# A DCNv3 layer ahead of an attention layer: position weights summed on GpSimd, and a new order of the work

## The chip, the cores and the metric

The kernel runs on one core of a Trainium2 chip. The time is the device time of one execution in microseconds (us). Three executions of the kernel before took 3407.39, 3409.13 and 3413.03 us, with a median of 3409.13 us. A core has five engines, each with a queue that it works through in order: TensorE (PE in the profile; its weight loads are PEld), VectorE (DVE), ScalarE (ACT), GpSimd (POOL) and SyncE (SP), which here issues most DMAs.

## The reference, cut to what matters

An image batch `x` of 2 x 512 x 64 x 64 floats goes through two layers, each added to its input. Layer 0, which alone is changed, is a deformable convolution (DCNv3) on the group-normed `x`:

```python
xproj = inp @ in_w + in_b                          # 512 -> 512, per pixel
x1 = conv 3x3, one filter per channel, of inp      # "depthwise", 9 taps
x1 = gelu(layernorm over the 512 channels(x1))
offset = x1 @ off_w + off_b                        # 16 groups x 9 points x 2
mask = softmax(x1 @ mask_w + mask_b over 9 points)
out = for each pixel and group: sum over 9 points of
      mask * bilinear sample of xproj at (point + offset)
x = x + out @ out_w + out_b
```

Layer 1 is full attention over 4096 pixels with 512 channels; the diff leaves it alone.

## The kernel before

**What is computed how.** Offsets are taken to stay below one pixel in size, so each sample reads at most a 5 x 5 neighbourhood. For each pixel and group the nine bilinear samples are therefore one weighted sum over 25 neighbours. These 25 *position weights* are what `weights` builds in the tile `aw` (128 pixels x 5 x 5 x 64, the 64 being 4 pixel blocks x 16 groups). Should an offset be larger, another path (not run here) recomputes everything.

**Chunks and stages.** Layer 0 works on 16 chunks of 512 pixels (8 rows of one image). Each chunk `i` goes through four stages, written as Python generators; a `yield` ends a step:

- `project(i)`: reads rows (SP), normalizes them on ACT into `xn` (one copy, 4 channel blocks `kb`), and multiplies by `in_w` on PE (`pq`, L789, 4 tiles), copied out by ACT (`xj`, L795).
- `features(i)`: the depthwise convolution. The first tap of each of the 4 channel blocks is an ACT instruction (L814); the other 8 x 4 taps are DVE `scalar_tensor_tensor` instructions (L820) that add to the tile `conv`. POOL sums the 4 blocks (L829, L831: `tot`), PE turns the sum into a mean over channels (`p_mean`, L836), DVE subtracts it (L841), ACT squares, POOL sums the squares (L847, L849: `sq`), PE takes the variance, ACT the root, DVE the reciprocal (L855) and product (L856), ACT the gelu (L860).
- `weights(i)`: PE multiplies by the offset and mask weights (`po`, L877, 4 tiles), DVE adds the bias into `o` (L882), ACT takes exp (L889), DVE forms the bilinear factors `tx` (L894, L895), ACT a relu that checks offsets (L901, it overwrites `o[:, 0:2]`), DVE the softmax sum and product (L904 to L909) and `my` (L912). Then come nine points: the first product goes straight into `aw`; each of the other eight is a DVE product into `pk` (L920, 128 x 576) and a DVE addition of `pk` into a 3 x 3 window of `aw` (L925). ACT copies all of `aw` into `at` in one instruction (L928), PE transposes it in 16 pieces (`p_tr`, L936) and ACT copies these to `awT` (L937).
- `sample(i)`: PE spreads the weights over the neighbourhood (`pb`, L965), ACT copies them to `bt` (L970), PE does the weighted sums (`pa`, L984), ACT copies them (`dT`, L995), PE multiplies by `out_w` (`py`, L1004, 4 tiles); DVE adds the input (`res`, L1009) and takes statistics for layer 1 (L1010).

**The order.** Inside `manual_schedule` the program's order is each engine's order. `period` writes the order of one round by hand: it interleaves `sample(i)` (called `m`), the tail of `sample(i-1)` (`y`), `weights(i+1)` (`w`), `features(i+2)` (`f`) and `project(i+3)` (`p`), the last transposes of `weights(i)` (`v`), and the first taps of `features(i+3)` (`g`). `more` takes one step of the statistics of image 1, whose input ACT fetches by DMA (L731, L744). Ahead of the 16 rounds stands the *fill*: stages of chunks 0, 1 and 2 in an order of their own. Chunks 14 and 15 have `next_to_last` and `last_period`.

**Buffers that matter.** In the pool of small tiles every tag has one buffer, so `pk` is one tile and `tot`, `sq` and `rstd` share another. PSUM tiles of the tag `mm` (`pq`, `py`, `po`, `p_tr`, `p_mean`) take turns in four buffers.

Of the kernel before, what the change touches and what calls it, by code (L numbers as in the profile page):

```python
# [13 lines left out]
ALU = mybir.AluOpType  # L14
# [515 lines left out]
LEAD = 4  # L530
SCORE_MAX = 6.0
# [43 lines left out]
def window_path(ctx: ExitStack, tc: tile.TileContext, t_in: dict, out: bass.AP, far: bass.AP, sums: bass.AP):  # L575
# [67 lines left out]
    with ExitStack() as l0:  # L643
# [111 lines left out]
        def project(i):  # L755
# [5 lines left out]
            raws = deque()  # L761

# [8 lines left out]
            for kb in range(3):  # L771
                read(kb)
# [5 lines left out]
            for kb in range(KB):  # L778
                nc.scalar.activation(
                    xn[:, kb, r0 : r0 + hi - lo, :], raws.popleft(),  # L780
                    AF.Identity, bias=bi[:, kb : kb + 1], scale=sc[:, kb : kb + 1],
                )
                if kb + 3 < KB:
                    read(kb + 3)
                yield
# [16 lines left out]
        def features(i):  # L802
# [9 lines left out]
            for kb in range(KB):  # L812
                dst, src, wt = tap_of(kb, 1)
                nc.scalar.activation(dst, src, AF.Identity, bias=dw_b[:, kb : kb + 1], scale=wt)  # L814
                if i < 2 or kb == KB - 1:
                    yield
            for kb in range(KB):
                for tap in (0, 2, 3, 4, 5, 6, 7, 8):
                    dst, src, wt = tap_of(kb, tap)
                    nc.vector.scalar_tensor_tensor(dst, src, wt, dst, ALU.mult, ALU.add)  # L820
                    if tap < 8:
                        yield

                if kb == 1:
                    if i == 1:
                        tot = io.tile([P, ROWS + 2, W], F32, name="raw", bufs=3).rearrange("p r c -> p (r c)")[:, :CH]
                    else:
                        tot = sm.tile([P, CH], F32, tag="tot", name="tot")
                    nc.gpsimd.tensor_add(tot, a[:, 0, :], a[:, 1, :])  # L829
                elif kb > 1:  # L830
                    nc.gpsimd.tensor_add(tot, tot, a[:, kb, :])  # L831
                yield

            def mean_over_c(tot):
                p = ps.tile([P, CH], F32, tag="mm", name="p_mean")
                nc.tensor.matmul(p, ones, tot, start=True, stop=True)  # L836
                return p

            mu = mean_over_c(tot)
# [3 lines left out]
            for kb in range(KB):  # L843
                nc.scalar.activation(f[:, kb, :], a[:, kb, :], AF.Square)
                if kb == 1:
                    sq = sm.tile([P, CH], F32, tag="tot", name="sq")
                    nc.gpsimd.tensor_add(sq, f[:, 0, :], f[:, 1, :])  # L847
                elif kb > 1:
                    nc.gpsimd.tensor_add(sq, sq, f[:, kb, :])  # L849
            yield  # L850
            var = mean_over_c(sq)
# [16 lines left out]
        def weights(i):  # L868
# [5 lines left out]
            for t in range(4):  # L874
                po = ps.tile([P, CH], F32, tag="mm", name="po")
                for kb in range(KB):
# [3 lines left out]
                    )  # L880
                yield
# [34 lines left out]
            for k in (4, 0, 1, 2, 3, 5, 6, 7, 8):  # L916
                kx, ky = divmod(k, 3)
                dst = aw[:, ky : ky + 3, kx : kx + 3, :]
                pk = dst if k == 4 else sm.tile([P, 3, 3, 4 * G], F32, tag="pk", name="pk")
# [4 lines left out]
                if k != 4:  # L924
                    nc.vector.tensor_add(dst, dst, pk)  # L925
                yield
            at = sm.tile([P, G, 4, 32], F32, tag="tx", name="at")
            nc.scalar.copy(  # L928
                at.rearrange("p g t w -> p w t g")[:, :NW], aw.rearrange("p y x (t g) -> p (y x) t g", t=4)
            )  # L930
            yield
# [101 lines left out]
        def period(y, v, m, w, f, g, p, more, last):  # L1033
# [5 lines left out]
            p()  # L1039
            y()  # L1040
            v(4)
            more()
            f(4)
            more()
            y()
            for taps in (9, 7, 6, 6):
                m(2)
                w()
                f(taps)
                w()  # L1050
                if taps in (7, 9):
                    more()
# [4 lines left out]
            f()  # L1057
            y()
            f()
# [8 lines left out]
            w(2)  # L1068
# [7 lines left out]
            for k, steps in enumerate((1, 2, 2, 2)):  # L1076
# [7 lines left out]
                if k == 2:  # L1084
                    more()
                if k < 3 and (k or not last):
# [3 lines left out]
                if k == 2:  # L1090
                    g()
            w()

        def next_to_last(y, v, m, w):

            y()
            w(8)
            v(4)
# [7 lines left out]
            w(2)  # L1106
# [54 lines left out]
        with tc.manual_schedule():  # L1161
# [7 lines left out]
            for t in range(4):  # L1169
                p0(2)  # L1170
                f0(8)
            border()
            more()
            p1(3)
            f1()
            next(products)
            p1()
            f1(2)
            next(products)
            p1()  # L1180
            f1()
            f1(6)
            f0(2)
            p1(4)
            f1(12)
            f0()
            p1(2)
            f0()
            p1()
            f0(2)  # L1190
            p1()
            f1(14)
            next(products)
            p2(5)
            f()
            for t in range(4):
                v()
                more()
                more()
                v()  # L1200
            fetch(0, 0)
            fetch(0, 1)
            f1()
            v()
            f1()
            v()
            p2(2)
            v(2)
            p2(2)
            v()  # L1210
            f1()
            v(3)
            p2(2)
            f1()
            p2()
            f1(2)
            p2()
            v(6)
            next(products)
            run(output_bias())  # L1220
            v()
            for i in range(NSEQ):
# [11 lines left out]
                period(y, v, m, w, f, g, Chain(project, i + 3), more, i + 3 == NSEQ)  # L1234
# [652 lines left out]
```

## Time and profile before

The profiled execution took 3413.08 us, and 3411.3 us of it lie between its first and last instruction. So it stands 3.95 us above the median of the three timed executions.

| stretch of the span | us | PE busy | DVE busy | ACT busy | POOL busy |
|---|---|---|---|---|---|
| fill, 20.0 to 158.9 | 138.9 | 91.7 | 119.2 | 55.9 | 29.1 |
| round with statistics of image 1, 230 to 301 | 71.0 | 66.2 | 66.6 | 53.9 | 13.0 |
| plain round, 646.8 to 714.5 | 67.7 | 64.5 | 62.7 | 53.9 | 13.1 |
| last rounds, 1125.1 to 1220 | 94.9 | 84.7 | 50.7 | 50.7 | 1.2 |
| layer 1, 1220 to 3411.3 | 2191.3 | 2071.2 | 1687.3 | 496.7 | 220.8 |

The instruction `my` (L912) stands once in each chunk; its starts lie 62.9, 70.8, 70.9, 71.3, 69.9, nine times 67.7 and 50.3 us apart. Where a row of the trace gives a start and a duration, the first number is the start in us from the span's beginning. A text in brackets is the idle time of the engine ahead of the instruction, with what ended it. "Busy" PE includes matmuls that stand in its pipeline, so a PE at 95% still has room.

### The profile page before, as it was taken

How to read it: one execution, taken by the hardware profiler on the slowest of the kernel's cores; microseconds unless marked ns; L12 is line 12 of the kernel's file. 1: busy time of each engine (PE TensorE's matmuls, PEld its weight loads, DVE VectorE, ACT ScalarE, POOL GpSimd, SP SyncE). 2: the span in 40 equal slices, each digit the busy share in tenths (PEclk: the TensorE clock that was granted, in tenths of full speed). 3: DMA queues.
4: the chain of work that ended last, by engine and by line, in shares of the span. 5: the costliest groups of instructions: out<-in, count | busy, mean ns of one | idle time of the engine just before them, and what ended most of it. 6: DMA issues, size and time to landing. Idle time of an engine off the chain costs nothing. (4 is left out here: it accounts for less than half of the span.)

```text
span 3411.3 us, 38291 instructions
## 1 busy us (share of the span) xinstructions
PE 3152.2 (92%) x14147; PEld 2265.2 (66%) x14147; DVE 2755.0 (81%) x3826; ACT 1349.5 (40%) x1802; POOL 435.7 (13%) x474
## 2 busy tenths in 40 slices
PE   5789999999999899899999999999899999999990
PEld 2355555555555567687787877887587787787880
DVE  8899999998999568786885976968697696885975
ACT  2477788788877533202213112023211202203105
POOL 2112111211121001001001010000101101001112
PEclk9799999999999999999999999999999999999995
DMA  6333443344333268758658667657866758658788
GB/s 227 104 99 116 136 125 111 93 127 128 101 97 117 98 233 268 235 181 236 190 167 222 197 192 207 202 189 247 256 196 193 208 185 236 185 170 223 240 296 356
DMA packets 238388, 629.98 MB, mean 185 GB/s; under 512 B 28112, under 2 KB 45136, under 8 KB 237168
## 3 DMA queue, kind: packets, MB, share of 16 engines
q1 hardware_dynamic: 181456, 431.07, 37.8%
q0 software_dynamic: 43936, 159.40, 18.0%
q10 hardware_dynamic: 12800, 36.97, 3.0%
q8 instruction: 114, 1.87, 0.2%
q14 instruction: 82, 0.67, 0.1%
HBM read 410.15 MB, written 124.91 MB: 157 GB/s over the span
## 5 line engine op out<-in xcount | busy, mean ns | idle before, releaser
L1501 PE MATMUL accy<-tt,v 128*128 128x256 f32 x2016 | 601.3, 380 | 0.8 <-DVE ct L1530 0.6
L1413 ACT ACTIVATE e<-pS 128x1024 f32<-128x1024 f32 x256 | 248.3, 1021 | 727.2 <-PE pS L1408 723.0
L1501 PE MATMUL accx<-e,v 128*128 128x256 f32 x1792 | 471.6, 386 | 0.0
L1501 PE MATMUL accy<-e,v 128*128 128x256 f32 x1792 | 461.3, 380 | 0.0
L820 DVE SCALAR_TENSOR_TENSOR conv<-xn,L_conv_dw_w_sb,conv 128x504 f32<-128x504 f32 (+1 forms) x512 | 409.4, 808 | 37.5 <-ACT conv L814 23.6
L1501 PEld LDWEIGHTS accy<-tt,v 128*128 128x128 f32 x2016 | 384.3, 191 | 53.8 <-DVE ct L1530 1.0
L1501 PEld LDWEIGHTS accx<-e,v 128*128 128x128 f32 x1792 | 334.2, 191 | 120.8 <-issue 80.6
L1501 PEld LDWEIGHTS accy<-e,v 128*128 128x128 f32 x1792 | 342.2, 191 | 46.1
L1480 DVE TENSOR_TENSOR tt<-e 128x256 f32<-128x256 f32 x448 | 187.7, 419 | 178.5 <-PE accy L1501 149.6
L1481 DVE TENSOR_TENSOR tt<-tt,e 128x512 f32<-128x512 f32 x448 | 310.0, 692 | 15.3
L1501 PE MATMUL accx<-tt,v 128*128 128x256 f32 x1008 | 301.3, 381 | 5.1 <-DVE tt L1480 5.1
L984 PEld LDWEIGHTS pa<-bt,patch 96*128 96x128 f32 x2048 | 249.6, 196 | 57.5 <-issue 34.9
L1408 PE MATMUL pS<-q,keys 64*128 64x512 f32 x1024 | 257.9, 623 | 15.3 <-ACT e L1413 15.3
L984 PE MATMUL pa<-bt,patch 96*128 96x128 f32 x2048 | 253.5, 281 | 7.7 <-ACT bt L970 6.3
L970 ACT COPY bt<-pb 96x1024 f32<-96x1024 f32 x124 | 235.1, 2009 | 58.1 <-PE pb L965 58.1
L789 PE MATMUL pq<-in_w,xn 128*128 128x512 f32 x512 | 240.5, 614 | 6.8 <-DVE o L882 4.6
L1004 PE MATMUL py<-dT,L_conv_out_w_sb 128*128 128x512 f32 x512 | 236.6, 607 | 4.8 <-ACT dT L995 4.8
L1506 ACT COPY u<-accx 128x256 f32<-128x256 f32 x56 | 20.8, 372 | 519.7 <-PE accx L1501 517.0
L1501 PEld LDWEIGHTS accx<-tt,v 128*128 128x128 f32 x1008 | 192.2, 191 | 32.0 <-DVE tt L1480 6.3
L877 PE MATMUL po<-om_w_pg,feat 128*128 128x432 f32 x512 | 204.8, 546 | 2.3 <-ACT feat L860 2.3
L995 ACT COPY dT<-pa 32x256 f32<-32x256 f32 x496 | 179.6, 362 | 66.0 <-PE pa L984 56.7
L1422 POOL DMA_DIRECT2D tot<-e x144 | 124.0, 887 | 583.5 <-DVE e L1398 277.7
(242 smaller groups left out, 4331.4 us busy)
## 6 DMA issues: line engine op xcount, KB each, us to landing
v<-wv SPq DMA_DIRECT2D x436, 448.0 KB
tot<-e POOLq DMA_DIRECT2D x176, 512.0 KB, 7.0
patch<-xt SPq DMA_DIRECT2D x256, 192.0 KB
v<-ww SPq DMA_DIRECT2D x56, 448.0 KB
wv<-vform SPq DMA_DIRECT2D x48, 512.0 KB
wv<-vsum SPq DMA_DIRECT2D x48, 384.0 KB
xt<-xj SPq DMA_DIRECT2D x128, 128.0 KB
res<-in_x SPq DMA_DIRECT2D x64, 256.0 KB
```

Source lines behind the costliest of these rows:

```text
L789: nc.tensor.matmul(pq, xn[:, kb, 1 + 2 * t : 3 + 2 * t, :].rearrange("p r c -> p (r c)"), in_w[:, kb, :], start=(kb == 0), stop=(kb == KB ...
L820: nc.vector.scalar_tensor_tensor(dst, src, wt, dst, ALU.mult, ALU.add)
L877: nc.tensor.matmul(po[:, : 3 * GP], f[:, kb, t * P : (t + 1) * P], om_w[:, kb].rearrange("p a k g -> p (a k g)"), start=(kb == 0), stop=(k ...
L970: copy(bt[:SN].rearrange("s g q d -> s d (g q)")[:, d0 : d0 + 4, :], pb[:SN])
L984: nc.tensor.matmul(pa[:, p], xp[:SN, p, cb * P : (cb + 1) * P], bt[:SN, 4 * cb : 4 * cb + 4, PX * s + p, :], start=True, stop=True,)
L995: copy(dst, src)
L1004: nc.tensor.matmul(py, out_w[:, kb, cb * P : (cb + 1) * P], dT[:, kb, :], start=(kb == 0), stop=(kb == KB - 1))
L1408: nc.tensor.matmul(p[:, a, :], keys[r, i, (2 * u + h) * P : (2 * u + h + 1) * P], c.q[r, qh, :], start=True, stop=True,)
L1413: nc.scalar.activation(e.rearrange("p a q -> p (a q)"), p.rearrange("p a q -> p (a q)"), AF.Exp)
L1480: nc.vector.tensor_sub(t[:, 0], x[:, 1], x[:, 3])
L1481: nc.vector.tensor_add(t[:, 1:3], t[:, 0].unsqueeze(1).to_broadcast([P, 2, HQ]), x[:, 0:3:2])
L1501: nc.tensor.matmul(out, v[:, blk, :], op, start=(first and g == 0), stop=(final and g == NG))
```

## The change

- **Position weights.** The eight additions of a product into `aw` (L925) go from DVE to POOL. The products no longer go into `pk`, but by turns into `o[:, 0]` and `o[:, 1]`, which are free by then: two buffers instead of one.
- **First taps.** For chunks 3 to 15 the first tap of the four channel blocks is a POOL `tensor_scalar` instead of an ACT instruction.
- **A block of taps.** For chunks 0 and 1 channel block 1 (`SHARED`) gets its eight other taps on POOL, each as a product into a scratch tile and an addition. There `tot` and `sq` are gone; PE takes the mean from the four blocks in four accumulating matmuls. Blocks run in the order 0, 2, 1, 3.
- **`at` in four parts.** Each part has a quarter of the groups, and is a step of its own.
- **Order.** A `po` tile is issued in two halves, with a `pb` between them. The transposes of a round come before the first `py` (`v(4)` ahead of `y()`), and the second `py` comes ahead of the mean. Four products follow on one another after the variance, then five more; two `at` parts come before the last `pa`, two after it, and the first taps of the next chunk after those. The fill has a new order, with six steps of `more` instead of nine, and more taps of chunk 2 within it.

```diff
+BLOCKS = 0, 2, 1, 3
+SHARED = 1
...
+            def share(kb):
+                x = io.tile([P, ROWS + 2, W], F32, name="raw", bufs=3)
+                for tap in (0, 2, 3, 4, 5, 6, 7, 8):
+                    dst, src, wt = tap_of(kb, tap)
+                    part = x[:, :ROWS, : dst.shape[2]]
+                    nc.gpsimd.tensor_scalar(part, src, wt, None, ALU.mult)
+                    nc.gpsimd.tensor_add(dst, dst, part)
+            fill = i < 2
+            for kb in BLOCKS if i < 3 else range(KB):
                 dst, src, wt = tap_of(kb, 1)
-                nc.scalar.activation(dst, src, AF.Identity, bias=dw_b[:, kb : kb + 1], scale=wt)
+                if i < 3:
+                    nc.scalar.activation(dst, src, AF.Identity, bias=dw_b[:, kb : kb + 1], scale=wt)
+                else:
+                    nc.gpsimd.tensor_scalar(dst, src, wt, dw_b[:, kb : kb + 1], ALU.mult, ALU.add)
+                if fill and kb == SHARED:
+                    share(kb)
...
+                parts = [tot[:, kb, :] for kb in range(KB)] if fill else [tot]
+                for k, x in enumerate(parts):
+                    nc.tensor.matmul(p, ones, x, start=(k == 0), stop=(k + 1 == len(parts)))
...
+                    if kb == 1:
+                        yield
                 yield
                 nc.vector.tensor_add(
                     o[:, :, :, t * G : (t + 1) * G].rearrange("p a k g -> p (a k) g"),
...
-                pk = dst if k == 4 else sm.tile([P, 3, 3, 4 * G], F32, tag="pk", name="pk")
+                pk = dst if k == 4 else o[:, e % 2].rearrange("p (y x) q -> p y x q", x=3)
...
-                    nc.vector.tensor_add(dst, dst, pk)
+                    nc.gpsimd.tensor_add(dst, dst, pk)
                 yield
             at = sm.tile([P, G, 4, 32], F32, tag="tx", name="at")
...
+            for b in range(4):
+                part = slice(4 * b, 4 * b + 4)
+                nc.scalar.copy(
+                    at.rearrange("p g t w -> p w t g")[:, :NW, :, part],
+                    aw.rearrange("p y x (t g) -> p (y x) t g", t=4)[:, :, :, part],
+                )
+                yield
...
+        def period(y, v, m, w, f, g, p, more, last, ahead, taps):
             p()
+            v(4)
             y()
-            v(4)
             more()
-            f(4)
+            f(ahead)
             more()
             y()
-            for taps in (9, 7, 6, 6):
-                m(2)
+            for k, count in enumerate(taps):
+                for _ in range(2):
+                    m()
+                    w()
+                f(count)
                 w()
...
-            f()
             y()
-            f()
+            f(2)
             m()
             p()
             w(2)
...
-            w(2)
+            w(4)
             p()
             y(2)
...
-            for k, steps in enumerate((1, 2, 2, 2)):
+            for k, steps in enumerate((2, 2, 1, 0)):
                 p()
                 w(steps)
...
                 if k == 2:
                     more()
+                    w(2)
                 if k < 3 and (k or not last):
                     m()
                 if k == 0:
                     f()
                 if k == 2:
+                    w(2)
                     g()
-            w()
...
         def next_to_last(y, v, m, w):
+            v(4)
             y()
-            w(8)
-            v(4)
+            w(12)
...
-            for t in range(4):
-                v()
-                more()
-                more()
-                v()
             fetch(0, 0)
             fetch(0, 1)
+            p2()
+            v(3)
             f1()
-            v()
+            for _ in range(3):
+                more()
+            p2(4)
+            v(3)
+            f()
+            v(3)
+            f(3)
+            v(3)
             f1()
...
+            more()
+            f(4)
+            v(4)
...
-                period(y, v, m, w, f, g, Chain(project, i + 3), more, i + 3 == NSEQ)
+                ahead, taps = (4, (9, 7, 6, 6)) if i else (0, (4, 6, 6, 6))
+                period(y, v, m, w, f, g, Chain(project, i + 3), more, i + 3 == NSEQ, ahead, taps)
```

## The prediction

> **What bounds the kernel now.** I read the busy shares by slice first: layer 0 is the first 1220 us, and there both PE (about 9 tenths) and DVE (9) are nearly full, so busy shares don't say which of them sets the pace. The waits within one plain round do. Columns: engine, tile and line that waited, who ended the wait, us in total, times, longest.
>
> ```profile
> PE p_mean L836 <- POOL tot L831: 1.2, 1, 1.2
> PEld p_tr L936 <- ACT at L928: 1.9, 1, 1.9
> DVE conv L820 <- ACT conv L814: 1.8, 1, 1.8
> DVE res L1009 <- PE py L1004: 1.4, 1, 1.4
> ```
>
> PE waits for DVE's sum, and DVE waits for PE's `py`: that is a loop over both engines. The timeline of the same round has the rest of it (start, duration, engine, line, names, count).
>
> ```profile
> 658.29 5.41 DVE L820 SCALAR_TENSOR_TENSOR conv<-xn,L_conv_dw_w_sb,conv 128x504 f32<-128x504 f32 x6
> 661.52 1.65 POOL L831 TENSOR_TENSOR tot<-tot,conv 128x512 f32<-128x512 f32 x1 [5.76 <-DVE conv L820]
> 664.15 4.64 DVE L820 SCALAR_TENSOR_TENSOR conv<-xn,L_conv_dw_w_sb,conv 128x504 f32<-128x504 f32 x6
> 668.93 1.27 POOL L831 TENSOR_TENSOR tot<-tot,conv 128x512 f32<-128x512 f32 x1 [5.77 <-DVE conv L820]
> 672.79 2.28 DVE L841 TENSOR_TENSOR conv<-conv,p_mean 128x2048 f32<-128x2048 f32 x1
> 692.69 0.69 DVE L1010 BATCH_NORM_STATS2 stats<-res 128x6 f32<-128x512 f32 x1
> 693.30 0.74 DVE L920 TENSOR_TENSOR pk<-my,tx 128x576 f32<-128x576 f32 x1
> 703.60 0.76 DVE L925 TENSOR_TENSOR aw<-aw,pk 128x576 f32<-128x576 f32 x1
> 706.17 3.09 DVE L820 SCALAR_TENSOR_TENSOR conv<-xn,L_conv_dw_w_sb,conv 128x504 f32<-128x504 f32 x4 [1.82 <-ACT conv L814]
> 707.05 3.60 PE L1004 MATMUL py<-dT,L_conv_out_w_sb 128*128 128x512 f32 x8
> 708.28 0.58 ACT L795 COPY xj<-pq 128x512 f32<-128x512 f32 x1
> 708.76 2.95 ACT L928 COPY at<-aw 128x1600 f32<-128x1600 f32 x1
> 710.68 0.75 DVE L1009 SCALAR_TENSOR_TENSOR res<-py,L_conv_out_b_sb,res 128x512 f32<-128x512 f32 x1 [1.42 <-PE py L1004]
> 711.76 1.97 PE L936 MATMUL p_tr<-ident,at 128*128 128x128 f32 x16 [1.11 <-ACT at L928]
> ```
>
> The reader is to see three things. One: the loop. PE goes from the mean (670.25) through three more `py`, `pa`, `pq` to the first `py` of the next round, done at 710.65 (40.4); DVE then runs `res` (710.68), 28 taps and POOL's last sum, and the next mean starts at 737.95 (27.3). 40.4 + 27.3 = 67.7, the round. Two: `at` starts at 708.76, 4.4 after the last addition (703.60 + 0.76 = 704.36), because ACT does four first taps and an `xj` before it; but the transposes come after `py`, so nobody on DVE waits for them. Three: six taps take 4.64 alone and 5.41 with a POOL addition beside them, and that addition takes 1.65 instead of 1.27. The `conv` L820 group has a median of 744 ns and a maximum of 1665: one tap stands still for 0.92.
>
> **The change in a plain round.** I follow DVE from the subtraction L841 (call its start S) to the next one, because the new order ties it to PE at a new place.
>
> 1. S to the end of the third statistics (L1010): 672.79 to 693.38 = 20.6 before. One addition goes (-0.76), two products come (+1.52). The third of these three needs the buffer of the first, so it waits for POOL's first addition. POOL's price: 1.27 for 128x512 with nothing in its way, by size 1.43 for 128x576. Without blocking the wait is about 0.8; with one product standing in POOL's way and one blocked it is up to 2.3. I take 1.7: 23.1 (22.2 to 23.7).
> 2. Five products and five POOL additions (seven DVE pairs before, 693.30 to 704.36). Each product but the first two needs the addition two before. At least 0.76 + 0.14 (from DVE's end to POOL's start, the tot row at 668.93) + 5 x 1.43 = 8.0. If each addition blocks the next product or waits for it, a pair takes about 2.0: 10.0. If product and addition never overlap: 5 x (0.76 + 1.43 + 0.25) = 12.2. I take 10.0, since DVE has nothing between the products but products with two inputs, the case of the 5.41 row.
> 3. ACT: four parts of `at`, with the four `dT` copies of the last `pa` (4 x 0.362 = 1.45) between the second and the third. One copy takes 2.95; a quarter is 0.74 if all of it goes by size, 0.89 with 0.2 fixed (`feat` squares: 512 elements 0.62, `e` 1024 elements 1.02, so 0.2 fixed). The last transposes need the PSUM buffer that the last `xj` frees (0.58), which now stands behind `at` in ACT's queue. 3.56 + 1.45 + 0.58 + 0.1 = 5.7 (5.0 to 6.9 if parts cost 1.2).
> 4. PE: the last four transposes 0.5, then the first `py`, which now stands behind them, 3.45, with hand-overs 4.1. Its DVE `res` waits for it, and behind `res` in DVE's queue stand 28 taps.
> 5. `res` to the next subtraction: 710.68 to 740.49 (672.79 + 67.7) = 29.8, unchanged; POOL's sums still contend.
>
> Sum: 23.1 + 10.0 + 5.7 + 4.1 + 29.8 = **72.7**, 5.0 over 67.7. With every low end 69.1 (+1.4), with every high end 76.6 (+8.9).
>
> What DVE sheds (8 x 0.758 = 6.1 us a round) so lies in the first half of the loop and is given back there as waits for POOL; a further 9.8 of ACT and PE (terms 3 and 4) comes between additions and taps, where before there were 6.3 (704.36 to 710.68). The first taps on POOL (4 of 0.54, by the 1600-element memset's 1436 ns, to 1.27, a whole addition) run while DVE waits for `py` anyway and cost nothing there; if `py` were early, they would start 0.9 after the last addition and each could block a tap. ACT loses 4 x 0.803 = 3.2 us of work at 53.9 busy in 67.7: hidden. The halved `po` may save up to 1.9 (pb to pa takes 18.35, of which 11.6 is `po` and 4.3 eight `pb` of 0.53), and `py` ahead of the mean 3.4, both on PE alone, which then waits at the mean instead. Memset, DMA issues and SP keep their places; SP issues hang on `xj` and `res`, moved by under 5 us against buffers a round ahead: nothing.
>
> A rule on this: the Trainium skill, "SBUF — State Buffer", section "Who interferes with whom", says that a DVE instruction with two SBUF inputs and a GpSimd instruction that reads SBUF exclude each other, the later one blocking for the whole of the earlier. The trace agrees on the kind, but the tap lost 0.92 of the addition's 1.27. By the rule to the letter, some four blocked products a round would lose 0.4 more each, 1.6 a round.
>
> **The other rounds.** The starts of `my` lie 70.8, 70.9, 71.3 and 69.9 apart in the four rounds with image 1's statistics. There three of six statistics fall into terms 1 to 5 outside the wait: 72.7 + 3 x 0.69 = 74.8 each, together 299.2 against 282.9: +16 (+2 to +32). Nine plain rounds: +45 (+13 to +80). The last round (50.3) has no taps behind `py`, only pairs spread among `pa`: 0 (-4 to +5).
>
> **The fill** and the first round. Five waits of DVE for image 1's data, with everything behind them:
>
> ```profile
> 108.69 0.69 DVE L744 BATCH_NORM_STATS2 gn_st<-early 128x6 f32<-128x512 f32 x1 [5.16 <-DMA early<-in_x]
> 111.04 0.69 DVE L744 BATCH_NORM_STATS2 gn_st<-early 128x6 f32<-128x512 f32 x1 [1.15 <-DMA early<-in_x]
> 112.85 0.69 DVE L744 BATCH_NORM_STATS2 gn_st<-xraw 128x6 f32<-128x512 f32 x1 [1.12 <-DMA xraw<-in_x]
> 118.94 0.70 DVE L744 BATCH_NORM_STATS2 gn_st<-early 128x6 f32<-128x512 f32 x1 [4.88 <-DMA early<-in_x]
> 120.30 0.69 DVE L744 BATCH_NORM_STATS2 gn_st<-early 128x6 f32<-128x512 f32 x1 [0.67 <-DMA early<-in_x]
> ```
>
> 13.0 us. Now three steps come together (their data are loaded long before) and two singly: most of it goes. Sixteen taps leave DVE (-12); sixteen POOL pairs come, each blocking about 0.92 + 0.45 (+22); twelve sums with their blocking go (-11): about -1. But POOL's block takes 8 x 2.75 = 22 us twice in a row, which sets when `xn` of chunk 1 is free and pushes chunk 0's variance and gelu back by about 5 us. Extra mean matmuls (24 x 0.43 = 10) lie on a PE with 47 us idle. Then the stalls of terms 1 to 3 once (some +3), and chunk 2's taps some 3 ahead. I take -9 (-20 to +8).
>
> Sum: 45 + 16 + 0 - 9 = +52, on 3413.1 of the profiled execution: 3465. That one stands 4 above the median of the three, so 3461; I write 3460.
>
> **The rivals.**
> A: PE becomes the bound, faster. With DVE out of the way the PE loop is 40.4 - 3.45 (`py` moved) + 1.75 (transposes) + 27.3 = 66.0. Rounds: 9 x -1.7, four with statistics at 67.4: -13; fill up to -20: about -48, 3361. For it: PE's 92% and the 4.9 us of waits in a round. It decides where `at`'s last part comes no later than PE is through `pq`: term 2 would have to be 5 us or less, 1 us for a pair, less than POOL's addition takes alone. Against it is that 1.27. So this needs PE work and DVE blocks that I misread.
> B: the loop holds, but at its low ends (POOL and DVE don't block each other in step), and the fill gives back 15 to 20: 13 + 2 - 18 = -3: 3395 to 3420.
> C: the two buffers are no help and every product waits for the addition before it: 76.6 a round: +80 + 32: 3510 to 3530.
>
> **How the numbers follow.** My forecast 0.62 (its own range 3420 to 3500), A 0.20, B 0.11, C 0.07. A measurement can tell about 0.2% (7 us) from no change. A is faster, B a third each way, C and the forecast slower: faster 0.24, same 0.04, slower 0.72. The range 3375 to 3505 leaves out the larger part of A and most of C.
>
> **What would show it.** Starts of `my` 72 to 73 apart; a wait of `res` L1009 for `py` of some 4 us and of `p_tr` for `at` of 2 to 5; `aw` additions on POOL of 1.4 to 1.9 with products of up to 1.8 between them; DVE busy in a round well below 62.7 plus waits; no DMA waits over 1 us at L744 in the fill. Wrong would be: rounds of 66 or less with PE waiting nowhere, or additions on POOL well under 1.2.

## The result, and the profile after

Five executions of the changed kernel have a median of 3481.17 us (3476.46 to 3488.05). Against the kernel before that is a ratio of **1.0217 (1.0206 to 1.0228)**: 72 us slower. The profiled execution took 3483.37 us with a span of 3481.5, 70.2 more than the span before.

Where these 70.2 lie is read from the starts of `my` (L933 now), with the start and the end of layer 0 and the end of the span:

| stretch | before | after | difference |
|---|---|---|---|
| start to the second `my` | 193.5 | 185.9 | -7.6 |
| four rounds with image 1's statistics | 282.9 | 296.3 | +13.4 |
| nine plain rounds | 609.5 | 668.9 | +59.3 |
| last distance between two `my` | 50.3 | 59.7 | +9.5 |
| last `my` to the end of layer 0 | 81.7 | 80.5 | -1.2 |
| layer 1 | 2193.4 | 2190.2 | -3.2 |

So most of the loss is in the plain rounds: 73.0 to 76.3 us each instead of 67.7. These are parts of one execution, and they vary. A kernel below that differs only in its next-to-last round took 196.9 to its second `my` and 659.6 for its nine plain rounds: the gain ahead of the second `my` is not a fixed one, and the plain rounds cost some 50 to 59.

The busy times of the whole span do not show where the loss comes from: DVE does 88 us less than before (2666.6, before 2755.0), and the kernel is 72 us longer. PE is busier by 76 (3227.7, before 3152.2) with only 24 more matmuls; something made the same matmuls longer. The waits of a round of 75.1 us, 700 to 775, say where DVE's time went (engine, tile and line that waited, who ended the wait, us, times, longest):

```profile
DVE res L1033 <- PE py L1028: 7.5, 1, 7.5
DVE o L941 <- POOL aw L946: 5.2, 4, 1.3
DVE conv L841 <- POOL conv L830: 3.5, 1, 3.5
PEld p_tr L960 <- ACT at L951: 2.9, 3, 1.8
```

Before, DVE's wait for `py` was 1.4 and its wait for a first tap 1.8. Now there are 16.2 us of waits. The timeline of the same round gives the chain that makes them (start, duration, engine, line, count, and in brackets the idle time ahead):

```profile
701.97 2.29 DVE L860 TENSOR_TENSOR conv<-conv,p_mean 128x2048 f32<-128x2048 f32 x1
723.71 0.69 DVE L1034 BATCH_NORM_STATS2 stats<-res 128x6 f32<-128x512 f32 x1
724.32 1.41 DVE L941 TENSOR_TENSOR o<-my,tx 128x576 f32<-128x576 f32 x2
725.21 9.43 POOL L946 TENSOR_TENSOR aw<-aw,o 128x576 f32<-128x576 f32 x5 [6.41 <-DVE o L941]
727.03 0.76 DVE L941 TENSOR_TENSOR o<-my,tx 128x576 f32<-128x576 f32 x1 [1.30 <-POOL aw L946]
734.67 1.62 ACT L951 COPY at<-aw 128x400 f32<-128x400 f32 x2 [0.55 <-POOL aw L946]
737.63 1.61 ACT L951 COPY at<-aw 128x400 f32<-128x400 f32 x2
738.57 0.66 PE L960 MATMUL p_tr<-ident,at 128*128 128x128 f32 x4 [1.56 <-ACT at L951]
739.27 0.59 ACT L798 COPY xj<-pq 128x512 f32<-128x512 f32 x1
739.91 1.12 PE L960 MATMUL p_tr<-ident,at 128*128 128x128 f32 x4 [0.68 <-ACT xj L798]
740.82 6.19 PE L1028 MATMUL py<-dT,L_conv_out_w_sb 128*128 128x512 f32 x8
747.04 0.75 DVE L1033 SCALAR_TENSOR_TENSOR res<-py,L_conv_out_b_sb,res 128x512 f32<-128x512 f32 x1 [7.51 <-PE py L1028]
```

The reader is to see two things. One: the last addition ends 32.7 us after the subtraction (734.64 - 701.97), about as early as before (31.6), but the first `py` is now behind the transposes, these behind `at`, and `at` behind the addition; so `res` starts 45.1 after the subtraction, where before it was 37.9 (710.68 - 672.79). Two: that first `py` takes 6.19, while the other three of the round take 3.60 each; over the nine plain rounds the first one takes 4.15 to 6.32. The busy time by stretch gives the reason (stretch, length, then PE, PEld, DVE, ACT, POOL busy with counts, the granted PE clock, DMA share, GB/s):

```profile
735.00:740.80 5.80, 3.49 (x18) 2.15 (x17) 4.00 (x4) 5.73 (x12) 5.43 (x5) 0.86 0.69 205
739.20:746.00 6.80, 6.12 (x12) 3.00 (x12) 0.33 (x1) 2.59 (x6) 1.43 (x1) 0.50 0.67 198
```

PE was busy for 3.49 of the 5.80 us to 740.8, waiting in between, and was granted half its clock in the stretch that follows; `py` fell into it.

### The profile page after: what moved, and what is told of

Same layout as the page of the kernel before. It is cut to its first block, busy times and chain, and to the rows that moved or that the text cites. A ratio compares the mean times of both kernels' runs of the same rounds, so it can differ in the third digit from the quotient of the medians.

```text
span 3481.5 us, 38488 instructions
## 1 busy us (share of the span) xinstructions
PE 3227.7 (93%) x14171; PEld 2279.8 (65%) x14171; DVE 2666.6 (77%) x3682; ACT 1323.0 (38%) x1799; POOL 751.9 (22%) x674
## 3 DMA queue, kind: packets, MB, share of 16 engines
q1 hardware_dynamic: 181456, 431.07, 37.9%
## 4 chain that ended last, share of the span: by engine, by line
PE 69%; DVE 14%; POOL 5%; DMA 4%; ACT 4%; issue 3%; SPq 0%; ACTq 0%; POOLq 0%; DVEq 0%
PE accy L1528 22%; PE accx L1528 17%; PE pS L1435 7%; PE py L1028 4%; POOL aw L946 4%; PE po L896 4%; PE pvy L1686 3%; DVE conv L841 3%; PE pb L989 2%; PE pa L1008 2%; PE pvx L1686 2%; PE pq L792 2%; PE pk L1758 1%; DMA wv<-vsum 1%; ACT at L951 1%
## 5 line engine op out<-in xcount | busy, mean ns | idle before, releaser
L841 DVE SCALAR_TENSOR_TENSOR conv<-xn,L_conv_dw_w_sb,conv 128x504 f32<-128x504 f32 x496 | 420.5, 855 | 52.3 <-POOL conv L830 37.2
L994 ACT COPY bt<-pb 96x1024 f32<-96x1024 f32 x124 | 243.9, 1975 | 162.3 <-PE pb L989 160.8
L946 POOL TENSOR_TENSOR aw<-aw,o 128x576 f32<-128x576 f32 x128 | 230.9, 1804 | 121.8 <-DVE o L941 114.2
L1028 PE MATMUL py<-dT,L_conv_out_w_sb 128*128 128x512 f32 x512 | 252.3, 640 | 1.4 <-ACT awT L961 1.4
L1449 POOL DMA_DIRECT2D tot<-e x144 | 124.0, 887 | 588.8 <-DVE e L1425 316.7
L1453 POOL DMA_DIRECT2D tot<-e x32 | 17.4, 544 | 974.0 <-DVE e L1425 835.8
L1533 ACT COPY u<-accx 128x256 f32<-128x256 f32 x56 | 20.8, 372 | 519.7 <-PE accx L1528 516.9
L896 PE MATMUL po<-om_w_pg,feat 128*128 128x432 f32 x512 | 217.0, 550 | 0.7 <-ACT feat L879 0.7
```

The lines of the kernel that those rows point to most:

```text
L896: nc.tensor.matmul(po[:, : 3 * GP], f[:, kb, t * P : (t + 1) * P], om_w[:, kb].rearrange("p a k g -> p (a k g)"), start=(kb == 0), stop=(k ...
L946: nc.gpsimd.tensor_add(dst, dst, pk)
L994: copy(bt[:SN].rearrange("s g q d -> s d (g q)")[:, d0 : d0 + 4, :], pb[:SN])
L1028: nc.tensor.matmul(py, out_w[:, kb, cb * P : (cb + 1) * P], dT[:, kb, :], start=(kb == 0), stop=(kb == KB - 1))
```

## The experiments

After this reading the theories were, in words:

- **The order**: `py` behind the transposes ties DVE's second half of the round to the end of the additions and of `at`. Its rival is **POOL's pace**: the additions simply take longer there, whatever the order.
- **The clock**: PE's small waits for `at` cost more than themselves, because the granted clock is halved behind them.
- **The lock**: DVE's products and POOL's additions hinder each other, and two buffers or three make no difference to that.
- **The PE loop**: once `py` is back in front, the next thing that binds is PE from the mean, over `po`, `pb`, `pa` and the second `py`, to the mean.
- **The fill**: its new order saves some 8 us by itself. The rival is that the DMA waits only move.

### Undoing the order, undoing the additions, and both

The first kernel is the changed one with `py` ahead of the transposes, the second has the additions on DVE, the third both.

```diff
 def period(...):
     p()
-    v(4)
     y()
+    v(4)
```
```diff
-                    nc.gpsimd.tensor_add(dst, dst, pk)
+                    nc.vector.tensor_add(dst, dst, pk)
```

> The changed kernel with one thing undone: in a round the first py stands ahead of the four transposes again. Theory 1 (the new order ties VectorE's 28 taps to the end of the at chain through py): res no longer waits for at. From the subtraction S, py is done at about S+36 by PE's own work, the last GpSimd addition at S+32.7, first taps and four taps end at S+37.6, then 29.8 to the next S: rounds of 67 to 68.5 instead of 75, the total 3390 to 3415. Theory 2 (the pace of the GpSimd additions alone makes the round long, wherever py stands): rounds stay at 72 or more, total above 3450.

> The changed kernel with the eight additions back on VectorE, all else as changed. Theory 1: the chain additions, at, transposes, py, res stays, but five pairs take 7.8 instead of 10.2 and the three pairs ahead about 1 more than now: rounds of 70 to 73 (the lower end if PE's clock stays full through py), total 3420 to 3455. Theory 2 (GpSimd's pace is the whole cause): rounds back at 67.7 or below, total at or under 3409.

> Both at once: py ahead of the transposes, additions on VectorE. Theory 1: neither the at chain nor GpSimd's pace is in the loop; PE's own work from the mean to py (about 37) plus res, 28 taps and the last sum (27 to 30) make rounds of 65 to 67, total 3365 to 3395, under the kernel before. Theory 2: the same as e2.

| kernel | median us | ratio to before | plain round | last addition | `res` |
|---|---|---|---|---|---|
| before | 3409.13 | | 67.7 | 31.6 | 37.9 |
| changed | 3481.17 | 1.0217 (1.0206 to 1.0228) | 75.1 (73.0 to 76.3) | 32.7 | 45.1 |
| `py` first | 3445.89 | 1.0108 (1.0090 to 1.0126) | 70.0 | 32.7 | 37.8 |
| additions on DVE | 3479.63 | 1.0210 (1.0193 to 1.0227) | 72 to 75 | 30.7 | 42.4 to 44.9 |
| both | 3443.02 | 1.0098 (1.0081 to 1.0115) | 70.3 | 30.7 | 37.2 |

The last two columns are times after the subtraction in a plain round. A ratio, here and below, is to executions of the kernel before that were timed along with it (medians of 3406.8 to 3409.1). One line in another place gives back 35 of the 72 us, and `res` is back where it was before. The round is not: 70.0 against the expected 67 to 68.5, and 70.3 against 65 to 67 with both undone, so something else holds it there, which is found below. Taking the additions off POOL gives back nothing that can be told, with either order: the last addition ends 2.0 earlier and nothing follows from it. The timeline of ACT in the kernel with the additions on DVE shows why; its subtraction starts at 697.0 and its last addition ends at 727.7:

```profile
727.57 0.58 ACT L798 COPY xj<-pq 128x512 f32<-128x512 f32 x1
728.05 1.48 ACT L1019 COPY dT<-pa 32x256 f32<-32x256 f32 x4
729.55 0.58 ACT L798 COPY xj<-pq 128x512 f32<-128x512 f32 x1
730.04 1.61 ACT L951 COPY at<-aw 128x400 f32<-128x400 f32 x2
```

`aw` is complete, but ACT has two `xj` and four `dT` ahead of `at` in its queue, so `at` starts 33.0 after the subtraction, as late as with POOL (32.7). POOL's pace is refuted as the cause of the loss.

### The additions alone on POOL

The kernel before, with nothing changed but the eight additions and their two buffers:

```diff
-            for k in (4, 0, 1, 2, 3, 5, 6, 7, 8):
+            for e, k in enumerate((4, 0, 1, 2, 3, 5, 6, 7, 8)):
...
-                pk = dst if k == 4 else sm.tile([P, 3, 3, 4 * G], F32, tag="pk", name="pk")
+                pk = dst if k == 4 else o[:, e % 2].rearrange("p (y x) q -> p y x q", x=3)
...
-                    nc.vector.tensor_add(dst, dst, pk)
+                    nc.gpsimd.tensor_add(dst, dst, pk)
```

> The kernel before with one part of the change alone: the eight additions on GpSimd, two product buffers; first taps, fill, order and at as before. Theory 1: the last addition ends at about S+34 instead of 31.6, but at starts at S+36 anyway behind the first taps and xj in ScalarE's queue, and py stays ahead of the transposes: plain rounds 67.7 again, total 3400 to 3415, neither gain nor loss. If GpSimd's additions cost by themselves: rounds of 70 or more, total above 3435. If shedding 6 us of VectorE is worth something by itself: rounds of 66 or less, total under 3390.

Measured: 3410.57, ratio 1.0008 (0.9999 to 1.0018); plain rounds 67.8. The last addition ends 35.4 after the subtraction, 3.8 later than before, and `at` still starts at 36.0 as before. The waits of a plain round, 674.2 to 742:

```profile
DVE o L920 <- POOL aw L925: 6.5, 5, 1.3
```

What DVE sheds (8 x 0.758 = 6.1) comes back as 6.5 of waits for POOL. So the largest edit of the change, taken alone, is worth nothing, either way: before, nobody waited for the end of the additions until ACT got to `at`, 4.4 us later.

### Keeping PE busy through its wait

The changed kernel with three more matmuls a chunk into the PSUM tiles that the transposes overwrite next, two ahead of the third tile and one ahead of the fourth. The order, and every wait for data, stays.

```diff
+                for _ in range((0, 0, 2, 1)[b]):
+                    nc.tensor.matmul(pt.rearrange("p g q -> p (g q)"), ident, in_w[:, 0, :], start=True, stop=True)
```

> The changed kernel with work added: PE does two matmuls (0.86 us each) into the transposes' PSUM tile ahead of the third group of transposes and one ahead of the fourth, where it now waits for at and xj; their results are overwritten. Theory 3 (these waits leave PE under about half busy for one 3.4 us window, the granted clock halves for the next one or two, and the py that all wait for takes 5.6 to 6.2 instead of 3.45): the clock stays at 1.0, py takes 3.0 between first and last start, rounds shrink by 1 to 2.5 to about 72.5, total 3450 to 3465 in spite of the added work. If py is slow for another reason (its data, DMA): rounds the same or 1 longer, 3480 to 3495.

Measured: 3476.97, ratio 1.0204 (1.0187 to 1.0221), so 4 below the changed kernel by the medians, with intervals that overlap. In the profiled execution the nine plain rounds took 657.7 instead of 668.9, and eight of them 73.0, with `py` at 3.60 in each. In the timeline of PE the added matmuls have the line of the transposes, and `py` is short again:

```profile
732.08 1.88 PE L960 MATMUL p_tr<-in_w,ident 128*128 128x512 f32 x4
733.83 0.66 PE L962 MATMUL p_tr<-ident,at 128*128 128x128 f32 x4
735.14 1.12 PE L960 MATMUL p_tr<-in_w,ident 128*128 128x512 f32 x2 [0.66 <-ACT xj L798]
736.10 0.60 PE L962 MATMUL p_tr<-ident,at 128*128 128x128 f32 x4
736.54 3.60 PE L1030 MATMUL py<-dT,L_conv_out_w_sb 128*128 128x512 f32 x8
```

The stretch that follows, in the columns of above, has the full clock:

```profile
735.00:745.00 10.00, 9.86 (x38) 4.72 (x38) 4.73 (x8) 5.24 (x7) 1.03 (x1) 1.00 0.77 265
```

More work on PE made the round shorter, 73.0 instead of the 75.1 shown above. The nine rounds alone would not show it: the same instructions as in the changed kernel took 659.6 in the kernel that differs only in its next-to-last round. But that trace settles it without any added work. In three of its plain rounds PE has the same two waits and keeps the full clock, and `py` takes 3.70 (the last row is such a round, in the columns of the stretches above):

```profile
599.74 0.66 PE L960 MATMUL p_tr<-ident,at 128*128 128x128 f32 x4 [1.58 <-ACT at L951]
601.07 0.66 PE L960 MATMUL p_tr<-ident,at 128*128 128x128 f32 x4 [0.68 <-ACT xj L798]
601.57 3.70 PE L1028 MATMUL py<-dT,L_conv_out_w_sb 128*128 128x512 f32 x8
563.14:635.32 72.18, 68.39 (x310) 38.74 (x309) 57.48 (x64) 51.50 (x71) 31.75 (x22) 1.00 0.33 105
```

These rounds take 72.2. So the clock theory holds: of the 668.9 of the changed kernel some 19 are the low clock (668.9 - 9 x 72.2), and in that other execution some 10. It is the smaller part of the 59, and how large differs from one execution to the next.

### A third product buffer

```diff
-                pk = dst if k == 4 else o[:, e % 2].rearrange("p (y x) q -> p y x q", x=3)
+                # by turns o[:, 0], o[:, 1] and a tile "pk"
```

> The changed kernel with three product buffers instead of two. Between products VectorE now waits 1.30 for GpSimd and a pair takes 2.06. Theory 4 (product and addition shut each other out while they read SBUF, so their times add up): VectorE waits less but products or additions get longer, the last addition still ends 32 to 33 after the subtraction S, the round and the total stay within 0.5 of the changed kernel's (73 to 75 a round). If the wait for the buffer alone sets the pace, additions run back to back at 1.43: last addition at S+30 to 30.5, rounds 2 shorter.

Measured: 3463.02 (two executions), ratio 1.0160 (1.0137 to 1.0184); plain rounds 71.5, two of them 73.0. From its timeline:

```profile
710.19 1.80 POOL L951 TENSOR_TENSOR aw<-aw,o 128x576 f32<-128x576 f32 x1 [6.41 <-DVE o L946]
710.63 3.85 DVE L946 TENSOR_TENSOR o<-my,tx 128x576 f32<-128x576 f32 x2
712.07 1.80 POOL L951 TENSOR_TENSOR aw<-aw,pk 128x576 f32<-128x576 f32 x1
714.40 1.96 DVE L946 TENSOR_TENSOR pk<-my,tx 128x576 f32<-128x576 f32 x1
717.71 1.40 POOL L951 TENSOR_TENSOR aw<-aw,pk 128x576 f32<-128x576 f32 x1
```

The waits for a buffer are gone, and a product that took 0.76 takes 1.96: what was a wait is now a product that stands still. A pair takes 1.88 instead of 2.06, and the last addition ends at 32.0 instead of 32.7. The lock theory fits as a mechanism. The round was expected to stay and lost 3.6 all the same: `at` comes 0.7 earlier, and in seven of the nine rounds the clock stayed full (`py` 3.70, `res` at 41.5). Against the 72.2 of the full clock above, 0.7 of the 3.6 is `at`, and 2.9 the clock. A small cause decides here whether a clock window falls on one side or the other.

### The mean ahead of the second `py`

The kernel with `py` first, and in addition the mean back ahead of the second `py`:

```diff
-    y()
-    f(2)
+    f()
+    y()
+    f()
```

> The changed kernel with two things undone: py ahead of the transposes, and the mean ahead of the second py as before. Without the second, rounds were 70.0: the last tap ended at S+63.6 as before, but the mean came at S+69.0 instead of 65.2. Theory 5 (the second loop goes through pb, the weights and pa to the mean, and the py now ahead of the mean lies in it): the mean moves up by 2.5 to 3.4, rounds 67.5 to 68.2, total 3405 to 3425. If halving po alone made the mean late: rounds stay above 69.

Measured: 3430.27, ratio 1.0063 (1.0046 to 1.0079); rounds of 68.5. So a second loop was behind the first. In the kernel with `py` first alone, the sum for the mean is done at 745.29, and the mean then stands behind a `py` until 749.27:

```profile
744.01 1.28 POOL L848 TENSOR_TENSOR tot<-tot,conv 128x512 f32<-128x512 f32 x1 [5.77 <-DVE conv L841]
745.83 3.60 PE L1028 MATMUL py<-dT,L_conv_out_w_sb 128*128 128x512 f32 x8
749.27 1.02 PE L855 MATMUL p_mean<-tot,ones_c 128*128 128x512 f32 x2
```

With the mean ahead it starts 66.8 after the subtraction instead of 69.0. What is left over the 67.7 stands in PE's timeline, first of this kernel, then of the one before:

```profile
721.76 1.11 PE L989 MATMUL pb<-awT,sel 25*96 25x256 f32 x8 [0.83 <-ACT awT L961]
722.80 1.72 PE L896 MATMUL po<-om_w_pg,feat 128*128 128x432 f32 x4
724.45 1.11 PE L989 MATMUL pb<-awT,sel 25*96 25x256 f32 x8
...
743.71 1.49 PE L1008 MATMUL pa<-bt,patch 96*128 96x128 f32 x11 [0.41 <-ACT bt L994]
```
```profile
714.56 1.14 PE L965 MATMUL pb<-awT,sel 25*96 25x256 f32 x16 [0.83 <-ACT awT L937]
715.62 3.17 PE L877 MATMUL po<-om_w_pg,feat 128*128 128x432 f32 x8
718.72 1.95 PE L965 MATMUL pb<-awT,sel 25*96 25x256 f32 x16
...
732.90 1.27 PE L984 MATMUL pa<-bt,patch 96*128 96x128 f32 x9
```

From the first `pb` to `pa` it is 21.95 with `po` in halves and 18.34 with whole `po`. Halves: eight times one `pb` and half a `po`, 1.04 + 1.65 = 2.69. Whole: four times two `pb` and a `po`, of which the two `pb` together take only 1.0 to 1.9. That the halves cost the remaining 0.8 of a round is argued from these rows; no kernel undid them alone.

### The fill alone, and what it moves

The fill of the changed kernel, with the block of taps on POOL, in front of the rounds of the kernel before:

```diff
-                    if kb == 1:
+                    if kb == 1 and i == 0:
                         yield
...
-            for b in range(4):
+            for b in range(4 if i == 0 else 1):
```

(with `period`, `next_to_last`, the additions and the first taps as before). The next kernel adds one more step of `more` ahead of each of the first three rounds, and the third then takes the first taps of chunks 3 to 15 to POOL.

```diff
+                if i < 3:
+                    more()
                 period(...)
```
```diff
-                if True:
+                if i < 3:
                     nc.scalar.activation(dst, src, AF.Identity, bias=dw_b[:, kb : kb + 1], scale=wt)
```

> The changed fill (blocks of taps on GpSimd, its order, at of chunk 0 in four parts) with the rounds of the kernel before: additions on VectorE, first taps on ScalarE, whole po tiles, at in one copy, old order. Theory: rounds 67.7 as before; the first my at 124 to 126 instead of 130.6 and the second at 186 to 189 instead of 193.5, so 5 to 8 less: total 3400 to 3405. If the fill's gain is given back in the rounds with statistics of image 1 (three steps more there): 3407 to 3412.

> The changed fill with the rounds of the kernel before, as in the run with the fill alone, and one more step of the statistics of image 1 ahead of each of the rounds 0, 1 and 2, so that the three steps that left the fill are made up early. Theory 6 (the fill is 7 us faster, and the run with the fill alone gave that back because the group-norm chain at the end of the statistics moved to a place where VectorE waits 3.5 and 5.8 for it): no such waits, rounds 4 to 6 back at 70 and 67.7, total 3399 to 3404. If the fill itself gains nothing: 3406 to 3412.

> The same, with the first taps of chunks 3 to 15 on GpSimd as in the change. Theory 1: taps start 2 earlier and at 1 to 3 earlier, but res still waits for py, which PE sets: rounds 67.5 to 67.8, no gain, 3399 to 3405. If ScalarE's queue ahead of at sets the round: 66 to 67, 3380 to 3395. If GpSimd's reads hold up VectorE's taps: 68.5 or more, above 3412.

| kernel | median us | ratio to before | rounds after the second `my` |
|---|---|---|---|
| fill alone | 3410.81 | 1.0011 (1.0001 to 1.0020) | 70.2 70.1 70.1 71.3, 74.1 70.7, then 67.7 |
| with `more` ahead | 3410.79 | 1.0009 (1.0000 to 1.0018) | 73.0 74.9 72.7 69.9, then 67.7 |
| with first taps on POOL | 3421.58 | 1.0038 (1.0025 to 1.0052) | 72.9 74.8 72.7 68.2, then 67.7 to 70.8 |

The second `my` comes at 186.1 in the first, 7.4 before its place in the kernel before, and all of that is lost again. Three steps of image 1's statistics have left the fill for the rounds. In the fill-alone kernel DVE then waits in the chain of that group norm, 9.3 us in all, as its timeline shows:

```profile
495.80 0.16 DVE L629 TENSOR_TENSOR gn_var<-gn_gm,gn_p 128x4 f32<-128x4 f32 x1 [3.51 <-PE gn_p L626]
501.76 0.18 DVE L633 RECIPROCAL gn_sc<-gn_var 128x4 f32<-128x4 f32 x1 [5.80 <-ACT gn_var L630]
```

With `more` ahead of the rounds it waits for the data instead. Its waits from 190.2 to 410.8:

```profile
DVE gn_st L746 <- DMA early<-in_x: 8.0, 3, 4.1
DVE gn_st L746 <- DMA xraw<-in_x: 4.1, 2, 3.4
```

That is 12.1 us, where the kernel before had 13.0 in its fill and 0.8 in these rounds. The expectation that the fill's gain stays is refuted: in this kernel the DMA waits moved into the rounds and kept nearly all of their size. The changed kernel itself has no such DMA wait in its rounds; from 185.9 to 483 DVE waits there for POOL (20.8 for additions, 8.9 for first taps) and ahead of `res` (18.7), and later in the group norm's chain (2.96 and 4.92).

First taps on POOL cost 11 us and not nothing. Some rounds take 67.7 and some 69.3, with the same instructions. The rows of PE at the mean, in a long round and in a short one, in the timeline of this kernel:

```profile
671.54 2.07 PE L855 MATMUL p_mean<-tot,ones_c 128*128 128x512 f32 x2 [2.24 <-POOL tot L848]
...
740.84 1.12 PE L855 MATMUL p_mean<-tot,ones_c 128*128 128x512 f32 x2 [2.28 <-POOL tot L848]
```

The wait is the same, 2.2 to 2.3; in the long round the clock falls behind it (granted 0.55 from 671.0 to 674.5), in the short one it does not (1.00 from 740.0 to 744.0). The mean, the next `py` and the variance are then late by 1 to 2. All nine plain rounds agree: the trace has six drops of the clock in them, one just ahead of the subtraction of each of the six long rounds (69.1 to 70.8) and none in the three of 67.7. POOL reading beside DVE's taps, which the expectation had for a number like this one, is not the cause, as the short rounds have the same first taps on POOL.

### The second `py` ahead of the mean, with whole `po`

If it is this wait at the mean, a `py` should be put into it. The same kernel, in a period that has the transposes behind the first `py` and `po` whole:

```diff
-    f()
     y()
-    f()
+    f(2)
```

> The same again, with the second py ahead of the mean as in the change, but po whole and the first py ahead of the transposes. Theory 5: PE gets through whole po tiles and pb pairs in 18.4 instead of 22, so the py ahead of the mean delays it by only 1 to 2 while it takes 3.45 out of the way from the mean to the next py: rounds of 66 to 67.3, total 3380 to 3400. If any py ahead of the mean costs what it takes: rounds of 68.5 to 70, above 3412.

Measured: **3401.61, ratio 0.9988 (0.9979 to 0.9997)**, the fastest of all kernels here, if only by 6 us. Two rounds of it, in columns as above:

```profile
660.00:727.00 67.00, 64.51 (x310) 38.40 (x310) 63.43 (x72) 50.93 (x68) 19.14 (x13) 1.00 0.36 114
727.00:794.00 67.00, 64.52 (x311) 38.39 (x310) 63.41 (x72) 50.90 (x68) 19.12 (x13) 1.00 0.37 114
```

The clock stays full, and every plain round but one is 67.0. So the same edit, the second `py` ahead of the mean, costs 1.5 a round in the changed order, where PE reaches that `py` after the sum is done (745.83 against 745.29), and gains 0.7 or more here, where PE had waited 2.2 for the sum. The two kernels differ in more than that, in the halves of `po` and in the engine of the additions, so that the early or late PE decides is argued from these rows.

### The last round

The changed kernel's last distance was 59.7 instead of 50.2. Its waits stand in PE's timeline, at the transposes, with `py` and `po` behind them:

```profile
1177.93 1.97 PE L960 MATMUL p_tr<-ident,at 128*128 128x128 f32 x8 [13.83 <-ACT at L951]
```

```diff
 def next_to_last(y, v, m, w):
-    v(4)
     y()
     w(12)
+    v(4)
```

> The changed kernel with the order of the next-to-last round undone: py and po ahead of the four transposes there. Theory 7 (PE stands 13.8 at the transposes there with py and po behind them, and then runs them at half clock): the last distance between my 49 to 52 instead of 59.7, total 3470 to 3476. If the last round is long because of GpSimd's additions: 58 or more, 3478 to 3485.

Measured: 3482.90, ratio 1.0220 (1.0205 to 1.0236); the distance is 56.9 and not the 49 to 52 expected, the total the same. PE's waits from 1154 to 1211:

```profile
PE py L1028 <- ACT dT L1019: 12.2, 2, 7.4
```

PE now waits nearly as long (12.2) for `dT`, the copy of the last `pa`, which is behind the first two `at` parts in ACT's queue, and these are behind the additions. So the four parts hold back `py` by two ways, and undoing one shows the other. The additions' engine is not what matters: with them on DVE the distance is 57.4 (58.3 with `py` first). That whole `at` brings the round back is shown only together with everything else (50.1 in the fill-alone kernel), so the cause of this part stays open.

## Why the prediction was right, and where it was not

The forecast was 3460 with a range of 3375 to 3505, slower. Measured was 3481, 21 above.

- **Term 1**, to the third statistics: 723.71 + 0.69 - 701.97 = 22.4, foretold 23.1. The wait for a buffer is 1.3 instead of 1.7.
- **Term 2**, five pairs: 10.2 (724.40 to 734.64), foretold 10.0. A pair is 2.06, product 0.76 and wait 1.30. Rival C's 12.2 is refuted.
- **Term 3**, `at`, `dT`, `xj`: 5.3 (734.64 to 739.91), foretold 5.7. A part takes 0.81, not 0.89.
- **Term 4**, transposes and `py`: **7.1, foretold 4.1. This is the term that failed.** `py` was put at 3.45, the full clock, for a PE that waits 1.56 and 0.68 just ahead of it. In the rounds that kept the full clock after the same waits the term is 4.2 (601.07 to 605.3) and the round 72.2, against the forecast's 72.7.
- **Term 5**, `res` to the next subtraction: 30.0, foretold 29.8.

The sum: 75.0 against 72.7 in a round of the low clock. Over nine rounds that made +59 instead of +45, and +50 in the other execution of the same rounds.

- **Rounds with statistics**: +13.4, foretold +16, and of the kind foretold: DVE waits for POOL and for `py` there, and nowhere for the data of the statistics.
- **Fill**: -7.6 up to the second `my`, foretold -9. That there would be no DMA waits over 1 us in it was right (one of 0.9). The gain is not a fixed one, though: in the kernel that differs only in the next-to-last round the second `my` comes at 196.9, 3.4 later than before. There the granted clock was 0.5 for 41 of the first 185 us instead of 20, and DVE waited 16.7 for `po` instead of 9.5. That the -7.6 fell near the -9 is in part luck.
- **Last round**: +9.5, foretold 0 (-4 to +5). The step looked only at what DVE has behind `py`. By the traces the cost is in ACT's queue, where `dT` is behind `at`, and in PE's, where `po` is behind the transposes; the one run on it undid only the second and did not bring the round back.
- **Halved `po`**, "may save up to 1.9": on the wrong side. It made PE's stretch 3.6 longer. In the rows of the kernel before a whole `po` takes 3.1 to 3.2, 12.5 for four and not 11.6, and eight `pb` take 5.8 and not 4.3, so there was little to save. The error was hidden, because in the changed order PE has waits to spare; it came out when `py` was moved back.
- **`py` ahead of the mean, 3.4 on PE alone, which then waits at the mean instead**: right in the changed order, where the mean is late anyway, and worth 1.5 a round as soon as `py` is first.
- **First taps on POOL, nothing**: the wait of 3.5 for them is inside the wait for `py`, as said. In the order of before they are not free: 11 us, through the clock.
- **Rival A** (PE bound, 66.0 a round) failed as the prediction put it: a pair takes 2.06 and not 1. Yet a round of 67.0 was found, by another order.

The sign rested on one argument, that a `py` behind the transposes ties DVE to the end of `at`. The move of that one line is worth 35 of the 72 us, so the argument is shown for half of the loss; of the rest, 16 are the mean behind the second `py`. The prediction has no such second loop; its sum came near all the same, because the first loop is the longer one and hides it. The remaining 21 of the kernel with both moved back are +12 in its nine plain rounds (72.8, 69.4, and seven of 68.5, against 609.5) and +8.3 in the last round.

## What to carry to other kernels

When an instruction is moved, ask what stands behind it in its own engine's queue and who waits for that; here the eight additions moved to an idle engine were worth nothing, and one line in the wrong place cost 35 us. Price a stretch of PE behind a wait at the clock that it will be granted, not at the one it had: filling the wait with any matmul, best with one that is needed anyway, can be worth more than the wait. A wait that leaves a stage is looked for in the next one, before it is counted as gained.

## What was not expected of the hardware

**Small waits of PE can halve its clock.** On a grid of 3.413 us that fits the places where the granted clock changes, the trace of the changed kernel has 25 drops to 0.5. All but one (in the fill, unexplained) stand behind a window in which PE was busy for 0.53 or less of the time; all other windows of 0.55 or more kept the clock, and three of 0.45 to 0.53 did too. The clock came back only behind windows of 0.81 and more, mostly after one or two. Each plain round has one drop, behind a window of 0.42 to 0.53. The kernel before has 19 drops, all behind windows of 0.53 or less, and none between 401.9 and 1105.0, in its plain rounds. The edge is not as sharp in every trace: with first taps on POOL there are drops behind windows of 0.59, 0.60 and 0.68, in the fastest kernel behind one of 0.81, and eight of the fourteen traces have one in the fill behind a full window. The Trainium skill, "TensorE: Matmul & The Clock Gate", section "What's actually happening", lets the half rate follow an idle window of about 3.4 us. The length agrees; but in the plain rounds no such window was idle, and a wait of 1.6 us within it, or one of 1.1 to 1.3 with one of 0.7, went ahead of the drop. Where the two waits fell into two windows, as in the round of 72.2 shown above (busy 0.66 and 0.64), the clock stayed.

**DVE and POOL take turns.** With two product buffers DVE waits 1.30 for an addition, with three its product takes 1.96 instead of 0.76: the pair costs 1.9 to 2.1 either way, where the parts alone take 0.76 and 1.40. The addition itself takes 1.97 with a product in its way.

**Two small matmul groups in a row are cheaper than two apart.** Two `pb` together took 1.0 to 1.9, one between two halves of `po` 1.04. Why is open.
